# Attention and mixture of experts on one core: the opening of the kernel written out by hand on four engines, and the later key tiles prepared two by two

## The chip, the core and the metric

The kernel runs on one core of a Trainium2 chip. The metric is the device time of one execution in microseconds (us); lower is better. The core has five engines that work side by side: TensorE (PE, matrix products and transposes, with its weight loads shown as PEld), VectorE (DVE), ScalarE (ACT), GpSimd (POOL), and SyncE (SP), which here only issues transfers. Each works through its own queue in order and waits on semaphores for the others.

## The reference

There are 2 batches of 1024 tokens of width 256, all in float32. A small conditioning vector gives six rows for each batch: shifts, scales and gates.

```python
mod = (silu(c) @ wmod).reshape(2, 6, 1, -1)
sa, ca, ga, sb, cb, gb = (mod[:, i] for i in range(6))   # then |ga|, |gb| >= 0.25
h = layernorm(x) * (1 + ca) + sa
xn = layernorm(h) * g_norm
q = l2norm(heads(xn @ Wq) * 16) * 4            # 16 heads of 128
k, v = split(xn @ Wkv)                         # one key and one value head for all
k = l2norm(k) * 4
o = softmax(q @ k.T) @ v
x = x + ga * (layernorm(merge(o) @ Wout) * g_out)
h = layernorm(x) * (1 + cb) + sb
x = x + gb * moe(h)                            # 8 experts, the best 2 for each token
```

## The kernel before

Tokens lie in 16 tiles of 128 (8 for each batch). The attention runs over 4 blocks of 512 query tokens. In a block every head goes over 8 key tiles; one such step is a score matmul (L478), an exponential on ACT (L482), a matmul with the values (L493) and a running sum on DVE (L498). `attention` walks 128 steps, with the scores two steps ahead (`AHEAD`), and at given steps it calls other work that `besides` holds: `at(h, j, f)` puts `f` ahead of step `h * 8 + j`. For block 0 the first sixteen steps are laid out so that two heads go over the first four keys and then over the last four (L809 to L811).

A tile gets its keys in stages. `prep_norm` makes both layer norms on DVE: statistics (L187, L188), then L357 and L360, statistics again, then L367. The inverse root of each is taken on POOL in `rsqrt`, by a scale (L177) and a power (L178). `key_value` transposes the tile on PE (L377), copies it out on ACT with `g_norm` as its scale (L379), and multiplies it by the key and value weights (L384). `normalised_keys` squares the keys on ACT (L399), takes `rsqrt` on POOL and scales them on DVE (L403); `prep_key` transposes them (L420) and copies them to `kT` (L421). Queries come in units of one token tile by four heads: `Queries.make` multiplies (L441) and calls `normalised` (square on ACT L343, sum on DVE L344, `rsqrt` on POOL, product on DVE L347), and `turn` transposes them (L455) and copies them out (L464).

Before the attention starts, lines 777 to 802 prepare the first four tiles: their norms by pairs, their keys, and group 0 of the queries (heads 0 to 3) of block 0. `warm` (L768) issues matmuls of ones whose results nobody reads. Tiles 4 to 7, the other half of the first batch's keys, are prepared one by one beside steps 0 to 5.

Nothing fixes the order of instructions on an engine except the order in which the program names them, dependencies, and a scheduler that fills each engine's queue at build time from what it holds to be ready. `tc.issue_after(ins)` makes what it encloses stand behind `ins` on the engine of `ins`.

Three buffers (`ps_s`) in PSUM hold scores, two (`ps_o`) hold outputs and three (`ps_m`) hold everything else. Outside the beginning the keys of tiles 8 to 15 are still made one by one beside heads 8 to 15 of block 0.

Of the kernel before, what the change touches and what calls it, by code (L numbers as in the profile page):

```python
# [55 lines left out]
def tile_adaln_attention_moe(  # L56
# [75 lines left out]
    wmod_in = wmod.rearrange("(c p) n -> p c n", p=P)  # L132
    wq_in = wq.rearrange("(c p) n -> p c n", p=P)
    nc.sync.dma_start(out=cT_sb, in_=cT.rearrange("(c p) b -> p c b", p=P))
    for t in range(PAIR):
        nc.sync.dma_start(out=xs[:, t, :], in_=xt[:, t, :])
    nc.sync.dma_start(out=wmod_sb[:, :, : 2 * D], in_=wmod_in[:, :, : 2 * D])
    for t in range(PAIR, QT):
        nc.sync.dma_start(out=xs[:, t, :], in_=xt[:, t, :])
    nc.sync.dma_start(out=gn_col, in_=g_norm.rearrange("(c p) -> p c", p=P))  # L140
    nc.sync.dma_start(out=wkv_sb, in_=wkv.rearrange("(c p) n -> p c n", p=P))
# [33 lines left out]
    def rsqrt(out, src, scale, add):  # L175

        nc.gpsimd.tensor_scalar(out, src, scale, add, ALU.mult, ALU.add)  # L177
        latest["pool"] = nc.gpsimd.tensor_tensor(  # L178
            out, out, minus_half[:, : out.shape[1]], ALU.pow
        ).ins  # L180
# [47 lines left out]
    with ExitStack() as attn:  # L228
# [109 lines left out]
        def normalised(src, n, scale, name):  # L338


            sq = work.tile([P, n, DH], FP, tag="sq", name=f"sq_{name}", bufs=1)
            rn = small.tile([P, n], FP, tag="rn", name=f"rn_{name}")
            nc.scalar.activation(sq, src, AF.Square)  # L343
            nc.vector.tensor_reduce(rn, sq, AX.X, ALU.add)  # L344
            rsqrt(rn, rn, 1.0 / ROOT_SCALE**2, L2_EPS / (scale * ROOT_SCALE) ** 2)
            vn = work.tile([P, n, DH], FP, tag=f"vn{n}", name=f"vn_{name}")
            nc.vector.tensor_tensor(  # L347
                vn, src, rn.unsqueeze(2).to_broadcast([P, n, DH]), ALU.mult
            )
            return vn  # L350

        z_of, kn_of = {}, {}
# [16 lines left out]
            )  # L369
            z_of[t] = z  # L370

        def key_value(t, pool, tag):

            z = z_of.pop(t)
            tp = ps_m.tile([P, DC, P], FP, tag="mm", name=f"tp_{t}")
            for c in range(DC):
                nc.tensor.transpose(tp[:, c, :], z[:, ts(c, P)], ident)  # L377
            for c in range(DC):
                nc.scalar.activation(  # L379
                    hT[:, t, c, :], tp[:, c, :], AF.Copy, scale=gn_col[:, c : c + 1]  # L380
                )
            kv = pool.tile([P, 2, DH], FP, tag=tag, name=f"kv_{t}")
            for c in range(DC):
                nc.tensor.matmul(  # L384
                    kv.rearrange("p a d -> p (a d)"),
                    hT[:, t, c, :],
                    wkv_sb[:, c, :],
                    start=(c == 0),
                    stop=(c == DC - 1),
                )  # L390
            nc.scalar.copy(vs[:, t, :], kv[:, 1, :])
            return kv

        def normalised_keys(tiles, kvs):

            rn = small.tile([P, QT], FP, tag="rn", name=f"rnk_{tiles[0]}")[:, : len(tiles)]
            for i, kv in enumerate(kvs):
                sq = work.tile([P, HG, DH], FP, tag="sq", name=f"sqk_{tiles[i]}", bufs=1)
                nc.scalar.activation(sq[:, 0, :], kv[:, 0, :], AF.Square, accum_out=rn[:, i : i + 1])  # L399
            rsqrt(rn, rn, 1.0 / ROOT_SCALE**2, L2_EPS / ROOT_SCALE**2)  # L400
            for i, kv in enumerate(kvs):
                kn = work.tile([P, DH], FP, tag="vn1", name=f"vnk_{tiles[i]}")
                nc.vector.tensor_scalar(kn, kv[:, 0, :], rn[:, i : i + 1], None, ALU.mult)  # L403
                kn_of[tiles[i]] = kn
# [7 lines left out]
            norm_again(t, h, mv, rs, 0)  # L412

        def prep_kv(t):
            normalised_keys([t], [key_value(t, ps_m, "mm")])

        def prep_key(t):

# [8 lines left out]
        class Queries:  # L427


            def __init__(self, blk):  # L430
                self.blk = blk
                self.groups = []
                self.units = [(g, i) for g in range(NG) for i in range(QT)]
                self.made = []

            def make(self, pool=ps_m, tag="mm"):
# [13 lines left out]
            def turn(self, only_act=False):  # L450

                g, i, qn = self.made.pop(0)
                tp = ps_m.tile([P, HG, P], FP, tag="mm", name=f"qp_{self.blk}_{i}_{g}")
                for j in range(HG):
                    nc.tensor.transpose(tp[:, j, :], qn[:, j, :], ident)  # L455
                if i == 0:
                    self.groups.append(
                        big.tile([P, HG, QB], FP, tag="qT", name=f"qT_{self.blk}_{g}", bufs=NG + 1)
                    )
                dst = self.groups[g][:, :, ts(i, P)]  # L460
                if i % 2 and not only_act:
                    nc.vector.tensor_copy(dst, tp)
                else:
                    nc.scalar.copy(dst, tp)  # L464

            def head(self, h):
                return self.groups[h // HG][:, h % HG, :]

        def attention(blk, q, steps, besides):
# [5 lines left out]

            def score(h, j):
                s = ps_s.tile([P, QB], FP, tag="s", name=f"s_{blk}_{h}_{j}")
                nc.tensor.matmul(  # L478
                    s, kT[:, ts(b * NJ + j, P)], q.head(h), start=True, stop=True
                )  # L480
                p = work.tile([P, QB], FP, tag="p", name=f"p_{blk}_{h}_{j}", bufs=4)
                nc.scalar.activation(p, s, AF.Exp)  # L482
                probs[h, j] = p

            def gather(h, j):
                p = probs.pop((h, j))
                if j == 0:
                    outs[h] = ps_o.tile([P, QB], FP, tag="o", name=f"o_{blk}_{h}")
                    sums[h] = work.tile(
                        [P, QB], FP, tag="sum", name=f"sum_{blk}_{h}", bufs=HG + 1  # L490
                    )
                    probs[h] = p
                nc.tensor.matmul(  # L493
                    outs[h], vs[:, b * NJ + j, :], p, start=(j == 0), stop=(j == NJ - 1)
                )
                if j:
                    first = probs.pop(h) if j == 1 else sums[h]
                    latest["vector"] = nc.vector.tensor_tensor(sums[h], first, p, ALU.add).ins  # L498
                if j == NJ - 1:
                    nc.scalar.copy(q.head(h), outs.pop(h))  # L500
# [273 lines left out]
                )  # L774


        q = Queries(0)
        pairs = [list(range(t, t + PAIR)) for t in range(0, QT, PAIR)]
        first = [statistics(small, [xs[:, t, :] for t in ts2], PAIR, f"p{ts2[0]}") for ts2 in pairs]
        warm(3, "a")  # L780
        modulate_in(0)
        warm(5, "b")
        second, hs = [], {}
        for ts2, (mv, rs) in zip(pairs, first):
            both = work.tile([P, QB], FP, tag="p", name=f"h_{ts2[0]}", bufs=4)
            for i, t in enumerate(ts2):
                hs[t] = both[:, ts(i, D)]
                norm_in(t, hs[t], mv, rs, i)
            second.append(statistics(small, [hs[t] for t in ts2], PAIR, f"n{ts2[0]}"))
        for n, (ts2, (mv, rs)) in enumerate(zip(pairs, second)):  # L790
            for i, t in enumerate(ts2):
                norm_again(t, hs[t], mv, rs, i)
            normalised_keys(ts2, [key_value(t, ps_o, "o") for t in ts2])
            for t in ts2:
                q.make(ps_s, "s")
            if n:
                for t in ts2:
                    q.turn(True)
            for t in ts2:
                prep_key(t)  # L800
        for t in ts2:
            q.turn(True)

        HALF = NJ // 2
        settle = None
        for blk in range(NBLK):
            steps = [(h, j) for h in range(HEADS) for j in range(NJ)]
            if blk == 0:
                steps[: 2 * NJ] = [  # L809
                    (h, j + k) for k in (0, HALF) for h in range(2) for j in range(HALF)  # L810
                ]  # L811
            besides = {n: [] for n in range(len(steps))}

            def at(h, j, f, *a):
                besides[h * NJ + j].append(lambda: f(*a))

            after = Queries(blk + 1) if blk + 1 < NBLK else None
            for h in range(HEADS):
                src = q if h < HEADS - HG else after
                if src is not None:  # L820
                    at(h, 0, src.make)
                    at(h, 4, src.turn)
            if settle is not None:
                for i in range(QT):
                    at(1 + i, 2, settle.logits, i)
                at(1 + QT, 2, settle.weights)
                at(1 + QT, 4, count, blk - 1, filled[0], work, ps_m, "mm")
            if blk == 0:
                for i, t in enumerate(range(QT, TPB)):
                    at(0, i, prep_norm, t)  # L830
                    at(0, i + 1, prep_kv, t)
                    at(0, i + 2, prep_key, t)
                for b in range(B):
                    at(2 + b, 3, gate_a, b)
                    at(2 + b, 6, gate_b, b)
                at(4, 4, tables)
                at(5, 3, modulate_moe, 0)
                at(5, 6, modulate_in, 1)
# [272 lines left out]
```

## Time and profile before

| | us |
|---|---|
| runs shown, median of 3 (lowest to highest) | 1354.47 (1352.8 to 1355.57) |
| the profiled execution | 1353.75 |
| its span, first to last instruction | 1352.0 |
| PE busy in the span | 1322.1 (98%) |
| DVE, ACT, POOL busy | 685.4, 489.4, 229.1 |
| first score matmul starts | 41.55 |

The span is what the profile sees; 1.75 us of the profiled execution lie around it. The chain of waits that ended last is followed back from the last instruction, and PE holds 93% of it. "PEclk" is the share of full clock that TensorE was granted. Matmuls of float32 show as two records each, and the ends of matmul records are modelled, so their durations overlap; spacing from start to start is the safer reading: 0.86 us for a matmul of 512 columns at full clock, 0.43 us for one of 256. Timelines and chains give the start and the length of each piece in us from the start of the span, with the engine, the line of the program and what is written from what.

### The profile page before, as it was taken

What the parts mean: (1) busy time and instruction counts of PE and PEld (TensorE: products, weight loads), DVE (VectorE), ACT (ScalarE), POOL (GpSimd) and SP (SyncE); (2) the same over time, 40 slices, a digit from 0 to 9 for tenths busy, and PEclk for the clock granted to TensorE, in tenths of its full rate; (3) what the DMA queues carried; (4) which work ended last, traced back from release to release, by engine and by line L of the source; (5) the groups of instructions that cost most, each with busy time, mean ns of one, the idle gap of its engine ahead of it and who ended that gap; (6) DMA issues with size and microseconds to landing.
All of it is one profiled execution on the core that took longest, in us unless ns stands there. A gap on an engine that the chain in (4) does not pass through costs nothing.

```text
span 1352.0 us, 12731 instructions
## 1 busy us (share of the span) xinstructions
PE 1322.1 (98%) x4024; PEld 686.6 (51%) x4024; DVE 685.4 (51%) x1380; ACT 489.4 (36%) x954; POOL 229.1 (17%) x325
## 2 busy tenths in 40 slices
PE   7899999999999999999999999999999999999995
PEld 3444444446644444447444444457444444476774
DVE  6356655544535554542636353544546544437645
ACT  2433344442243433330343333321333333304442
POOL 4200212110100111000100000001000224003633
PEclk9899999999999999999999999999999999999998
DMA  7000000000003410000001200100001013013435
GB/s 245 1 0 19 13 15 18 1 31 32 1 1 121 93 32 0 31 1 32 0 1 32 86 32 0 32 1 32 1 0 32 26 54 103 31 32 119 135 123 194
DMA packets 46322, 59.18 MB, mean 44 GB/s; under 512 B 10672, under 2 KB 32432, under 8 KB 46256
## 3 DMA queue, kind: packets, MB, share of 16 engines
q1 hardware_dynamic: 42512, 48.08, 11.6%
q0 software_dynamic: 3744, 10.29, 2.1%
q8 instruction: 33, 0.54, 0.2%
q14 instruction: 33, 0.27, 0.1%
HBM read 39.69 MB, written 18.66 MB: 43 GB/s over the span
## 4 chain that ended last, share of the span: by engine, by line
PE 93%; DVE 2%; DMA 2%; POOL 2%; issue 1%; ACT 0%; SPq 0%; POOLq 0%; DVEq 0%; ACTq 0%
PE s L478 32%; PE o L493 32%; PE pr L547 8%; PE q L441 8%; PE su L928 3%; PE sy L959 2%; PE qp L455 2%; PE den L507 1%; DMA out_dram<-res 1%; PE kv L384 1%; PE ap L944 1%; PE xp L913 1%; POOL rn_q L178 0%; PE lg L625 0%; DMA wmod_sb<-in_wmod_dram 0%
## 5 line engine op out<-in xcount | busy, mean ns | idle before, releaser
L478 PE MATMUL s<-qT,kT 128*128 128x512 f32 x1024 | 525.5, 595 | 0.1
L493 PE MATMUL o<-p,vs 128*128 128x512 f32 x1024 | 522.7, 593 | 0.0
L482 ACT ACTIVATE p<-s 128x512 f32<-128x512 f32 x512 | 305.6, 597 | 502.4 <-PE s L478 497.3
L498 DVE TENSOR_TENSOR sum<-sum,p 128x512 f32<-128x512 f32 x384 | 264.5, 689 | 180.2 <-ACT p L482 175.5
L493 PEld LDWEIGHTS o<-p,vs 128*128 128x128 f32 x1024 | 193.5, 190 | 233.2 <-issue 232.1
L478 PEld LDWEIGHTS s<-qT,kT 128*128 128x128 f32 x1024 | 187.4, 191 | 206.0 <-issue 204.1
L177 POOL TENSOR_SCALAR rn_q<-rn_q 128x4 f32<-128x4 f32 x64 | 14.0, 219 | 721.1 <-DVE rn_q L344 706.0
L441 PE MATMUL q<-wq_sb,rows 128*128 128x512 f32 x256 | 121.0, 596 | 0.0
L547 PE MATMUL pr<-wout_sb,qT 128*128 128x256 f32 x512 | 112.7, 381 | 0.0
L547 PEld LDWEIGHTS pr<-wout_sb,qT 128*128 128x128 f32 x512 | 96.7, 190 | 18.8 <-issue 4.3
L498 DVE TENSOR_TENSOR sum<-p,p 128x512 f32<-128x512 f32 x64 | 44.2, 691 | 113.4 <-ACT p L482 113.3
L344 DVE TENSOR_REDUCE rn_q<-sq_q 128x4 f32<-128x512 f32 x64 | 43.8, 684 | 84.0 <-ACT sq_q L343 83.9
L178 POOL TENSOR_TENSOR rn_q<-rn_q,minus_half 128x4 f32<-128x4 f32 x64 | 83.3, 1302 | 5.3
L441 PEld LDWEIGHTS q<-wq_sb,rows 128*128 128x128 f32 x256 | 49.1, 192 | 60.5 <-issue 50.5
L347 DVE TENSOR_TENSOR vn_q<-q,rn_q 128x512 f32<-128x512 f32 x64 | 44.2, 690 | 58.2 <-POOL rn_q L178 58.2
L343 ACT ACTIVATE sq_q<-q 128x512 f32<-128x512 f32 x64 | 38.2, 597 | 75.1 <-PE q L441 70.8
L523 DVE TENSOR_TENSOR qT<-qT,wide 128x512 f32<-128x512 f32 x64 | 42.2, 690 | 44.5 <-DMA wide<-spread 44.2
L515 DVE RECIPROCAL rden<-den 128x512 f32<-128x512 f32 x16 | 53.7, 3358 | 20.0 <-PE den L507 20.0
L928 PE MATMUL su<-w_sb,xT 128*128 x184 | 62.9, 462 | 0.2
L970 POOL DMA_INDIRECT results<-ysb,x x46 | 46.4, 1009 | 54.2 <-DVE ysb L967 37.9
L455 PEld LDWEIGHTS qp<-ident,vn_q 128*128 128x128 f32 x256 | 32.3, 143 | 37.3 <-issue 31.2
L959 PE MATMUL sy<-w2s,sactT 128*128 x184 | 47.2, 380 | 0.0
(160 smaller groups left out, 763.4 us busy)
## 6 DMA issues: line engine op xcount, KB each, us to landing
wide<-spread SPq DMA_DIRECT2D x64, 256.0 KB
x<-sorted_x SPq DMA_DIRECT2D x46, 130.0 KB
y<-results SPq DMA_DIRECT2D x16, 256.0 KB
sorted_x<-zero SPq DMA_DIRECT2D x1, 4030.0 KB
w_sb<-in_w_dram SPq DMA_DIRECT2D x2, 1408.0 KB
wout_sb<-in_wout_dram SPq DMA_DIRECT2D x1, 2048.0 KB
out_dram<-res SPq DMA_DIRECT2D x16, 128.0 KB
sorted_x<-zero SPq DMA_DIRECT2D x1, 1950.0 KB
```

The costliest lines, as they stand in the source:

```text
L178: latest["pool"] = nc.gpsimd.tensor_tensor(out, out, minus_half[:, : out.shape[1]], ALU.pow).ins
L441: nc.tensor.matmul(q.rearrange("p h d -> p (h d)"), hT[:, self.blk * QT + i, c, :], wq_sb[:, c, ts(g, QB)], start=(c == 0), stop=(c == DC ...
L455: nc.tensor.transpose(tp[:, j, :], qn[:, j, :], ident)
L478: nc.tensor.matmul(s, kT[:, ts(b * NJ + j, P)], q.head(h), start=True, stop=True)
L482: nc.scalar.activation(p, s, AF.Exp)
L493: nc.tensor.matmul(outs[h], vs[:, b * NJ + j, :], p, start=(j == 0), stop=(j == NJ - 1))
L498: latest["vector"] = nc.vector.tensor_tensor(sums[h], first, p, ALU.add).ins
L515: nc.vector.reciprocal(rden, den)
L547: nc.tensor.matmul(ps, q.head(h)[:, ts(i, P)], wout_sb[:, h, :], start=(h == 0), stop=(h == HEADS - 1),)
L928: nc.tensor.matmul(u, self.xT[:, c, :], w1_flat[:, c * I2 :][:, bass.ds(at, I2)], start=(c == 0), stop=(c == DC - 1),)
L959: nc.tensor.matmul(y, self.actT[:, c, :], w2_flat[:, c * D :][:, bass.ds(at, D)], start=(c == 0), stop=(c == 1),)
L970: ins = nc.gpsimd.indirect_dma_start(out=results[self.i], out_offset=bass.IndirectOffsetOnAxis(ap=self.x[:, TO : TO + 1].bitcast(I32), axi ...
```

## The change

The loads that open the kernel are reordered: the first third of `wmod` (what `modulate_in` needs) is issued ahead of all four first tiles of `x`, instead of between the second and the third. The rest of the beginning is rewritten.

- The four helpers of a tile are split, so that transposing, multiplying, copying the values and measuring lengths can be named apart (`transposed`, `key_value`, `value`, `key_lengths`, `lengths`, `scaled`). With `both`, half of a tile's copy out after the transpose is on DVE and half on ACT.
- The preparation of tiles 0 to 3 stands in `tc.manual_schedule` for PE, DVE, ACT and POOL: on each of these engines the instructions inside run in the order in which they are written. The norms of tiles 4 and 5 are written in between.
- Group 0 of the queries is made by two token tiles and two heads at a time (`some_queries`, into a buffer of `ps_s`; `turn_some`). Heads 0 and 1 are finished for all four tiles before the first score; heads 2 and 3 of the lower two tiles are multiplied ahead of it (`q_more`) and finished beside step 3; those of the upper two tiles are made beside step 9 and turned beside step 13.
- An exponential of one column is issued early on ACT. `warm` has 3, 7 and 1 matmuls in place of 3 and 5.
- Tiles 6 and 7 have their norms traced at step 0, behind the last query product of the beginning on DVE. The keys of tiles 4 and 5, then of 6 and 7, are made in pairs, each piece behind the attention's latest matmul on PE (`on_tensor`).
- The first sixteen steps go over keys in three parts: 0 to 3, 4 and 5, 6 and 7, for two heads each.
- Group 1 of block 0's queries is made beside steps 11, 16, 21 and 25 instead of 0, 8, 16 and 24.

```diff
-    for t in range(PAIR):
-        nc.sync.dma_start(out=xs[:, t, :], in_=xt[:, t, :])
     nc.sync.dma_start(out=wmod_sb[:, :, : 2 * D], in_=wmod_in[:, :, : 2 * D])
-    for t in range(PAIR, QT):
+    for t in range(QT):
         nc.sync.dma_start(out=xs[:, t, :], in_=xt[:, t, :])
...
+                if both and c:
+                    nc.vector.tensor_scalar(
+                        hT[:, t, c, :], tp[:, c, :], gn_col[:, c : c + 1], None, ALU.mult
+                    )
+                else:
+                    nc.scalar.activation(
+                        hT[:, t, c, :], tp[:, c, :], AF.Copy, scale=gn_col[:, c : c + 1]
+                    )
...
         q = Queries(0)
...
+        def some_queries(tiles, h0):
+            u = ps_s.tile([P, PAIR, PAIR, DH], FP, tag="s", name=f"q_{tiles[0]}_{h0}")
+            for i, t in enumerate(tiles):
+                for c in range(DC):
+                    nc.tensor.matmul(
+                        u[:, i].rearrange("p h d -> p (h d)"),
+                        hT[:, t, c, :],
+                        wq_sb[:, c, h0 * DH : (h0 + PAIR) * DH],
+                        start=(c == 0),
+                        stop=(c == DC - 1),
+                    )
+            return u.rearrange("p i h d -> p (i h) d")
+
+        def turn_some(tiles, h0, vn):
+            tp = ps_m.tile([P, PAIR, PAIR, P], FP, tag="mm", name=f"qp_{tiles[0]}_{h0}")
+            for h in range(PAIR):
+                for i in range(PAIR):
+                    nc.tensor.transpose(tp[:, h, i, :], vn[:, i * PAIR + h, :], ident)
+            dst = q.groups[0][:, h0 : h0 + PAIR, tiles[0] * P : (tiles[0] + PAIR) * P]
+            nc.scalar.copy(dst.rearrange("p h (i k) -> p h i k", k=P), tp)
...
+        with tc.manual_schedule(engines=engines):
+            warm(3, "a")
+            x_low = statistics(small, [xs[:, t, :] for t in low], PAIR, "p_low")
+            x_high = statistics(small, [xs[:, t, :] for t in high], PAIR, "p_high")
+            modulate_in(0)
+            none = small.tile([P, 1], FP, name="none", bufs=1)
+            nc.scalar.activation(none, ones[:, 0:1], AF.Exp)
+            warm(7, "b")
+            h_low = first_norm(low, *x_low)
+            n_low = statistics(small, h_low, PAIR, "n_low")
+            h_high = first_norm(high, *x_high)
+            second_norm(low, h_low, *n_low)
+            n_high = statistics(small, h_high, PAIR, "n_high")
+            for t in low:
+                transposed(t, True)
+            kv_low = [key_value(t, ps_o, "o") for t in low]
+            for t, kv in zip(low, kv_low):
+                value(t, kv)
+            rk_low = key_lengths(low, kv_low)
+            second_norm(high, h_high, *n_high)
+            x_mid = statistics(small, [xs[:, t, :] for t in middle], PAIR, "p_mid")
+            for t in high:
+                transposed(t, True)
+            q_low = some_queries(low, 0)
+            normalised_keys(low, kv_low, rk_low)
+            rq_low = lengths(q_low, HG, SCALE, "q_low")
+            kv_high = [key_value(t, ps_o, "o") for t in high]
+            for t in low:
                 prep_key(t)
-        for t in ts2:
-            q.turn(True)
-
-        HALF = NJ // 2
+            for t, kv in zip(high, kv_high):
+                value(t, kv)
+            rk_high = key_lengths(high, kv_high)
+            q_high = some_queries(high, 0)
+            both = work.tile([P, QB], FP, tag="p", name="h_mid", bufs=4)
+            h_mid = [both[:, ts(i, D)] for i in range(PAIR)]
+            norm_in(middle[0], h_mid[0], *x_mid, 0)
+            vn_low = scaled(q_low, HG, rq_low, "q_low")
+            rq_high = lengths(q_high, HG, SCALE, "q_high")
+            norm_in(middle[1], h_mid[1], *x_mid, 1)
+            turn_some(low, 0, vn_low)
+            q_more = some_queries(low, PAIR)
+            n_mid = statistics(small, h_mid, PAIR, "n_mid")
+            warm(1, "c")
+            vn_high = scaled(q_high, HG, rq_high, "q_high")
+            anchor = latest["multiplied"]
+            turn_some(high, 0, vn_high)
+            normalised_keys(high, kv_high, rk_high)
+            for t in high:
+                prep_key(t)
+            second_norm(middle, h_mid, *n_mid)
...
+        def on_tensor(f, *a):
+
+            with tc.issue_after(latest["tensor"]):
+                f(*a)
...
+        FIRST = ((0, NJ // 2), (NJ // 2, NJ // 2 + PAIR), (NJ // 2 + PAIR, NJ))
...
-                    (h, j + k) for k in (0, HALF) for h in range(2) for j in range(HALF)
+                    (h, j) for j0, j1 in FIRST for h in range(2) for j in range(j0, j1)
...
-                    at(h, 0, src.make)
-                    at(h, 4, src.turn)
+                    late = (11, 8, 5, 1)[h] if not blk and h < HG else 0
+                    at(h, late, src.make)
+                    at(h, late + 4, src.turn)
...
-                for i, t in enumerate(range(QT, TPB)):
-                    at(0, i, prep_norm, t)
-                    at(0, i + 1, prep_kv, t)
-                    at(0, i + 2, prep_key, t)
+                at(0, 0, norms_of_last)
+                at(0, 0, on_tensor, turn_rows, middle)
+                at(0, 1, on_tensor, keys_of, middle)
+                at(0, 3, finish_low)
+                at(0, 5, on_tensor, turn_keys, middle)
+                at(0, 5, on_tensor, turn_rows, last)
+                at(0, 6, on_tensor, keys_of, last)
+                at(1, 2, on_tensor, turn_keys, last)
+                at(1, 1, make_rest)
+                at(1, 5, turn_rest)
```

## The prediction

> **What bounds the kernel.** I read the chain of waits first: PE holds 93% of it. The page says the same:
>
> ```profile
> PE 1322.1 (98%) x4024; PEld 686.6 (51%) x4024; DVE 685.4 (51%) x1380; ACT 489.4 (36%) x954; POOL 229.1 (17%) x325
> ```
>
> The change touches the first 65 us, so I cut that stretch into windows (window: length, then busy us of PE, PEld, DVE, ACT and POOL with counts, the granted clock, DMA):
>
> ```profile
> 10.00:20.00 10.00, 8.46 (x27) 4.32 (x26) 8.69 (x30) 2.80 (x11) 4.81 (x11) 1.00 1.03 373
> 20.00:30.00 10.00, 7.46 (x24) 4.86 (x23) 5.98 (x14) 3.03 (x13) 5.78 (x13) 0.83 0.73 226
> 30.00:40.00 10.00, 4.89 (x21) 3.13 (x20) 5.82 (x16) 3.09 (x7) 5.55 (x12) 0.74 0.00 0
> 40.00:50.00 10.00, 10.00 (x23) 4.57 (x22) 2.95 (x5) 5.78 (x11) 2.21 (x4) 0.75 0.01 2
> 50.00:60.00 10.00, 8.94 (x32) 4.52 (x30) 3.32 (x8) 5.27 (x18) 2.48 (x6) 1.00 0.00 1
> ```
>
> PE idles until about 40, and from 20 to 45 much of what it does runs at half clock. A wider window, 200 to 320, has PE busy 120.00 of 120. So what is saved before the flow is dense is saved at the end, and no later event stands at a fixed time to take it back. PE's timeline gives the point where dense work starts (start, length, what, idle before):
>
> ```profile
> 36.27 1.09 PE L455 MATMUL qp<-ident,vn_q 128*128 128x128 f32 x4 [2.08 <-DVE vn_q L347]
> 38.97 1.09 PE L455 MATMUL qp<-ident,vn_q 128*128 128x128 f32 x4 [1.60 <-DVE mv_n L188]
> 39.85 1.92 PE L441 MATMUL q<-wq_sb,rows 128*128 128x512 f32 x2
> 41.55 3.59 PE L478 MATMUL s<-qT,kT 128*128 128x512 f32 x4
> ```
>
> The last line is two scores: 3.6 us where two cost 1.72 at full clock. What holds PE until then is in the chain, POOL and DVE in turn:
>
> ```profile
> 32.93 0.20 POOL rs_p L177
> 33.13 0.07 issue
> 33.20 0.54 POOL rs_p L178
> 33.74 0.08 issue
> 33.82 0.50 POOL rn_q L177
> 34.32 0.07 issue
> 34.39 1.02 POOL rn_q L178
> ```
>
> The query's inverse length waits behind tile 5's (`rs_p`), which no score needs yet. DVE likewise does norms of later tiles between pieces that PE waits for. The written order goes at this.
>
> **What must be done anyway.** By 65.43 tiles 0 to 7 are ready. From 39.85 to 65.43 are 25.6 us. PE lost 1.5 in gaps (0.48, 0.19, 0.62, 0.19, ahead of the `kp` transposes) and 2.5 to the half clock (0.85 on half a query unit, 1.66 on two scores). So 21.6 us of PE work at full clock.
>
> Work before 39.85 against work ahead of the new first score: both have `s_c`, four tiles' rows, values and keys. The new one makes three quarters of group 0 (not four: 1.72 fewer) and turns two quarters (not four: 2 x 0.44 fewer). That is 2.6 us left for later. If the first score starts at T, the work of 65.43 is done at T + 2.6 + 21.6 + stalls, and the gain is 65.43 - 24.2 - T - stalls = 41.2 - T - stalls.
>
> **T, part by part.** Durations are rows of before: statistics of a tile 0.55 (3.79 to 4.96 for two), norm pass 0.45 (two passes a tile), L367 0.35, L403 0.33, sum L344 0.62, product L347 0.66, square 0.6, copy out of four transposes 0.58, ACT values and lengths 0.17 + 0.37 a tile; POOL 1.15 for two columns and 1.45 for four, hops included.
>
> *The loads.* SP issues `wmod` second, at 1.30 instead of 2.26; five issues move past each other and none is added. It took 4.60 from issue to landing with 256 KB of `x` ahead of it, so at the latest 5.9. At the earliest 5.0: the first `x` tile needed 2.5 to its first use, and three more such tiles' worth take 0.4 each (`wmod` 6.86, next tile used 7.26). The four `x` tiles follow 0.4 apart, the last at 6.6 to 7.5 (before, used by 7.83). I carry 5.9 through the walk.
>
> *DVE from there.* Statistics of four tiles end 8.5; `one_ca` 8.94 (before 9.43). Norms of low 10.8, their statistics 11.9, norms of high 13.7, L367 of low 14.4, statistics of high 15.5. PE: `s_c` to 7.65, seven warm matmuls 6.02 to 13.67; then the first transposes at 14.1 (before 14.68). So the load order buys half a microsecond; the two extra warm matmuls (1.72) lie in PE idle time, and would cost only if L367 were done before 13.67.
>
> *Copies out on two engines.* DVE has two of 0.33 after its statistics, 15.5 to 16.16; ACT alone takes 1.14 for the four (15.16 to 16.3). This is worth nothing or a loss of 0.3 here, since DVE comes late; nearest row: L403, the same kind of operation from PSUM, 0.35.
>
> *Low keys and queries.* kv ends 17.2, the query product of heads 0 and 1 runs 17.65 to 19.4. DVE: L367 of high waits for POOL to 16.65, ends 17.35, statistics of tiles 4 and 5 to 18.45, two scales to 19.1, low keys scaled 19.45 to 20.1 (POOL's `rnk`, after ACT's lengths at 18.3), sum of low queries 20.24 to 20.86, norm of tile 4 to 21.76, product of low queries 22.32 to 22.98 (after POOL's four columns).
>
> *High.* kv of high needs the `ps_o` buffers that the low keys free: 19.9 to 21.6. Its queries 21.8 to 23.5, square 23.7 to 24.3, sum to 25.0, POOL to 26.45. DVE meanwhile does tile 5's norm and both tiles' statistics to 27.0: this later work overruns POOL by 0.55. Product 27.67, transposes 28.2, copy 28.4 to 29.0. **T is 29.0** with the late `wmod`, 28.1 with the early one; I take 28.8, nearer the row. DVE works 20 of those 23 us: it becomes the bound of the beginning.
>
> *The exponential ahead.* The table load is 1.28 us on ACT in both kernels; at 40.70 it hid under the slow score (waited for until 43.5), now it hides in ACT's gap before 14. Worth 0.
>
> *After T.* Each pair's rows, keys and `rsqrt` are spread over several steps. Two tiles' copies out take 1.17 of ACT, an exponential 0.6, and PE has a score and an output, 1.72, to cover them. The pieces that can stand bare are the transposes of tiles 6 and 7 (a third `ps_m` buffer waits for a copy of 0.3) and the key copies just ahead of score 12 (0.3 to 0.5). `q_more` holds one score buffer until its product: two remain, and a score needs one back after 0.6 of exponential, inside 1.72 of other work. Behind a waiting `on_tensor` piece stand the attention's matmuls, and behind those every exponential; before, four such waits cost 1.5. The bounds are 0 and 3; I take 1.0, since two pairs stop PE half as often as four tiles. Group 1 later is free: its last turn is two steps (1.7 to 3.4 us) ahead of use, against a copy of 0.6. `group`, `latest` and the split helpers add no instructions.
>
> *The clock.* It changed at 24.5, 27.9, 34.75 and 45.0: multiples of 3.4 apart. The stretch 21.1 to 24.5 had four transposes (0.44) and nothing else, and half clock followed. [...] That speaks against this change: from the warm matmul's end (26.5) to the first score (29.0) there are only transposes. [...] By the rows, windows of about a tenth busy halved the clock and none near a third is shown; a halving costs half of 3.4 us, 1.7. I take 0, and keep 1.7 for the range.
>
> Sum: gain 41.2 - 28.8 - 1.0 = 11.4. Against its own execution 1353.75 - 11.4 = 1342.3; that execution lies 0.7 under the median shown, so against the median **1343.0**.
>
> **Rivals.** A measurement tells about 0.2% (2.7 us) from no change.
>
> *A, the clock or the waits move along.* As above, but the gap before the first score fills a window (1.7 us), or norms of tiles 6 and 7 slip among the last DVE pieces, or step waits reach 3. For it: DVE's overrun already sits there. [...] 2 to 4 us less: about 1345.7.
>
> *B, everything early.* `wmod` lands at 5.0 and no step stalls: T 28.1, gain 13.1, 1341.4. Against: copies on ACT do compete.
>
> *C, the written order blocks and the time is longer.* In a fixed queue one late piece holds all behind it. If low and high don't overlap at all, one pair's way from its transposes to its queries' copy is 12.4 us (0.44, 0.6, 1.87, 1.08, 1.1, 0.66, 0.66, 1.72, 0.6, 0.62, 1.4, 0.66, 0.44, 0.58 in order); two make 24.9, the middle norms 5.1 and `q_more` with its warm matmul 2.6. From 14.1 that is T = 46.7, a loss of 6.5: 1361. It decides from T = 40.2, 11 us past my walk. Against: PE and ACT in the walk have room to work on one pair while POOL serves the other.
>
> *D, the order isn't kept or half works.* T near 34: 1348.5.
>
> **Chances.** Main 0.55, own range 1341.8 to 1344.6. A 0.22, B 0.13, D 0.06, C 0.04. The range 1340.5 to 1346.8 holds main, B and most of A, leaving out C, D and A's tail. Faster by over 0.2% 0.95 (all but C and a corner of D), within 0.02, slower 0.03.
>
> **What would show it.** First score at 28 to 29.5; last product of the beginning at about 27, with DVE the engine that sets it; PE gaps after the first score of about 1 in sum; clock 1.00 throughout from 5 us on. Score and output counts are unchanged, and the stretch from the end of tile 7's keys to the end is as long as before. Wrong: a first score after 31, a half-clock stretch after it, or PE gaps later than 65 us that before didn't have.

## The result and the profile after

The changed kernel takes 1346.34 us (median of 6 runs, 1345.55 to 1347.16), the kernel before 1353.32 beside it: a ratio of 0.9948, 95% interval [0.9937, 0.9958], or 7.0 us less. The forecast was 1343.0, 11.4 less than the runs then shown; the range of 1340.5 to 1346.8 holds the result near its upper end, where it had been stretched to take in most of rival A; the main case's own range, 1341.8 to 1344.6, does not reach it. The profiled span fell from 1352.0 to 1344.7.

The same windows after the change (length, busy us of PE, PEld, DVE, ACT and POOL, granted clock, DMA):

```profile
10.00:20.00 10.00, 9.16 (x36) 5.31 (x35) 8.43 (x28) 3.17 (x12) 3.67 (x8) 1.00 1.02 388
20.00:30.00 10.00, 8.02 (x39) 6.05 (x38) 7.58 (x21) 3.40 (x13) 4.84 (x9) 1.00 0.69 214
30.00:40.00 10.00, 8.53 (x27) 4.38 (x25) 6.43 (x18) 5.46 (x16) 4.21 (x10) 1.00 0.01 2
40.00:50.00 10.00, 8.27 (x24) 4.49 (x25) 2.65 (x4) 3.85 (x10) 0.95 (x1) 0.83 0.00 1
50.00:60.00 10.00, 10.00 (x32) 5.74 (x31) 3.43 (x8) 4.05 (x11) 0.94 (x3) 1.00 0.00 0
```

PE is dense 12 us earlier than before, but not from the first score on: 30 to 50 has a hole. PE's timeline shows both ends of it:

```profile
27.93 0.63 PE L822 MATMUL qp<-ident,vn_q_high 128*128 128x128 f32 x4 [1.52 <-DVE vn_q_high L351]
28.39 0.38 PE L440 MATMUL kp<-ident,vnk 128*128 128x128 f32 x2
29.23 1.98 PE L502 MATMUL s<-qT,kT 128*128 128x512 f32 x4 [0.46 <-ACT qT L824]
...
37.51 1.02 PE L517 MATMUL o<-p,vs 128*128 128x512 f32 x2
41.73 1.11 PE L822 MATMUL qp<-ident,vn_q_more 128*128 128x128 f32 x4 [3.20 <-DVE vn_q_more L351]
42.63 1.92 PE L502 MATMUL s<-qT,kT 128*128 128x512 f32 x2
44.34 1.41 PE L517 MATMUL o<-p,vs 128*128 128x512 f32 x2
45.59 1.02 PE L502 MATMUL s<-qT,kT 128*128 128x512 f32 x2
```

The first score starts at 29.23, against 41.55. After 37.51 PE waits 3.20 us for the product that the transposes of `q_more` need, at step 3, and then works slowly: from start to start the transposes take 0.90 (0.44 elsewhere), the score 1.71 and the output 1.25 (0.86 each), 1.7 us too many. The clock windows name the reason (third number from the end):

```profile
39.00:40.00 1.00, 0.00 (x0) 0.00 (x0) 0.81 (x2) 0.00 (x0) 0.62 (x2) 1.00 0.00 0
40.00:41.00 1.00, 0.00 (x0) 0.00 (x0) 0.02 (x1) 0.00 (x0) 0.95 (x1) 1.00 0.00 0
...
42.00:43.00 1.00, 1.00 (x5) 0.97 (x5) 0.00 (x0) 0.12 (x1) 0.00 (x0) 0.50 0.00 0
43.00:44.00 1.00, 1.00 (x2) 0.34 (x1) 0.00 (x0) 0.46 (x1) 0.00 (x0) 0.50 0.00 0
44.00:45.00 1.00, 1.00 (x2) 0.34 (x1) 0.00 (x0) 0.41 (x1) 0.00 (x0) 0.50 0.00 0
```

What held the product? POOL's timeline, and DVE's for the same stretch:

```profile
36.09 0.19 POOL L175 TENSOR_SCALAR rs_p<-mv_p 128x1 f32<-128x1 f32 x1 [1.55 <-DVE mv_p L186]
36.37 0.55 POOL L176 TENSOR_TENSOR rs_p<-rs_p,minus_half 128x1 f32<-128x1 f32 x1
37.00 0.19 POOL L175 TENSOR_SCALAR rnk<-rnk 128x2 f32<-128x2 f32 x1
37.27 0.70 POOL L176 TENSOR_TENSOR rnk<-rnk,minus_half 128x2 f32<-128x2 f32 x1
39.30 0.56 POOL L175 TENSOR_SCALAR rn_q_more<-rn_q_more 128x4 f32<-128x4 f32 x1 [1.32 <-DVE rn_q_more L345]
39.94 1.01 POOL L176 TENSOR_TENSOR rn_q_more<-rn_q_more,minus_half 128x4 f32<-128x4 f32 x1
```

```profile
38.01 0.61 DVE L420 TENSOR_SCALAR vnk<-kv,rnk 128x128 f32<-128x128 f32 x2 [2.00 <-POOL rnk L176]
38.53 0.67 DVE L345 TENSOR_REDUCE rn_q_more<-sq_q_more 128x4 f32<-128x512 f32 x1
39.13 0.68 DVE L522 TENSOR_TENSOR sum<-sum,p 128x512 f32<-128x512 f32 x1
40.98 0.69 DVE L351 TENSOR_TENSOR vn_q_more<-q,rn_q_more 128x512 f32<-128x512 f32 x1 [1.17 <-POOL rn_q_more L176]
```

The squares of `q_more` were ready at 36.3 (on ACT, 35.70 and 0.60 long). Their sum (L345) stands behind the keys' scales (L420) in DVE's queue, those wait for POOL's `rnk`, and on POOL `rs_p`, the norm of tile 8, which DVE first uses at 144.7, stands ahead of `rnk`. It is the pattern of the kernel before, moved to the first steps.

### The profile page after: what moved, and what is told of

It reads as the page before. It is cut to its first block, busy times and chain, and to the rows that moved or that the text cites. A ratio compares the mean times of both kernels' runs of the same rounds, so it can differ in the third digit from the quotient of the medians.

```text
span 1344.7 us, 12754 instructions
## 1 busy us (share of the span) xinstructions
PE 1320.7 (98%) x4046; PEld 688.4 (51%) x4046; DVE 686.7 (51%) x1384; ACT 488.2 (36%) x951; POOL 225.1 (17%) x313
## 3 DMA queue, kind: packets, MB, share of 16 engines
q1 hardware_dynamic: 42512, 48.08, 11.5%
## 4 chain that ended last, share of the span: by engine, by line
PE 94%; DVE 2%; DMA 2%; POOL 1%; issue 0%; ACT 0%; SPq 0%; POOLq 0%; DVEq 0%; ACTq 0%
PE s L502 32%; PE o L517 32%; PE q L462 8%; PE pr L571 8%; PE su L1069 4%; PE sy L1100 3%; PE qp L476 2%; PE den L531 1%; PE kv L396 1%; PE ap L1085 1%; PE xp L1054 1%; PE lg L649 0%; DMA y<-results 0%; DMA wide<-spread 0%; DMA xs<-in_x_dram 0%
## 5 line engine op out<-in xcount | busy, mean ns | idle before, releaser
L462 PE MATMUL q<-wq_sb,rows 128*128 128x512 f32 x240 | 112.8, 592 | 0.0
L345 DVE TENSOR_REDUCE rn_q<-sq_q 128x4 f32<-128x512 f32 x60 | 41.1, 685 | 84.4 <-ACT sq_q L344 84.2
L176 POOL TENSOR_TENSOR rn_q<-rn_q,minus_half 128x4 f32<-128x4 f32 x60 | 79.4, 1323 | 4.9
L462 PEld LDWEIGHTS q<-wq_sb,rows 128*128 128x128 f32 x240 | 45.5, 190 | 56.9 <-issue 46.4
L351 DVE TENSOR_TENSOR vn_q<-q,rn_q 128x512 f32<-128x512 f32 x60 | 41.4, 690 | 54.0 <-POOL rn_q L176 54.0
```

The source lines that it names most:

```text
L176: latest["pool"] = nc.gpsimd.tensor_tensor(out, out, minus_half[:, : out.shape[1]], ALU.pow).ins
L462: nc.tensor.matmul(q.rearrange("p h d -> p (h d)"), hT[:, self.blk * QT + i, c, :], wq_sb[:, c, ts(g, QB)], start=(c == 0), stop=(c == DC ...
```

## Experiments

The first four ran on a chip where the kernel before takes 1353.1; the others on chips where it takes 1358.1 and 1357.8. So times are compared as ratios to the kernel before on the same chip, and a first score is compared by its distance from the first transposes (`tp`), since the start of the kernel shifts by about 1 us from one execution to the next (the first `tp` of the changed text starts anywhere from 13.64 to 14.66).

**split_turn: only the transposes of step 3 go to step 7.**

```diff
-            turn_some(low, PAIR, normalised(q_more, HG, SCALE, "q_more"))
+            made["more"] = normalised(q_more, HG, SCALE, "q_more")
+
+        def turn_low():
+            turn_some(low, PAIR, made["more"])
...
                 at(0, 3, finish_low)
+                at(0, 7, turn_low)
```

> Only the transposes of the lower tiles' second query half move, from step 3 to step 7; their length and product stay traced at step 3. Theory S: what the forecast missed is one PE wait of 3.2 us ahead of these transposes (38.5 to 41.7) and the half-clock window that follows it (1.9 us). Then both go: 5.1 us less than the changed kernel's 1346.3, so 1341.2, no PE gap over 0.5 us after the first score and clock 1.00. Rival R: PE waits at step 3 for something that step 5 needs as well (the pair's keys, or a score buffer that the unfinished queries hold), so the wait moves on: at most 1.5 us less, about 1345, with a gap of 2 to 3 us at step 5 or 7.

Measured: 1341.59, ratio 0.9920 [0.9907, 0.9933]. PE's timeline at the old place and at the new one:

```profile
38.38 1.02 PE L517 MATMUL o<-p,vs 128*128 128x512 f32 x2
39.23 1.02 PE L502 MATMUL s<-qT,kT 128*128 128x512 f32 x2
...
48.49 0.60 PE L822 MATMUL qp<-ident,vn_q_more 128*128 128x128 f32 x4
48.92 1.02 PE L502 MATMUL s<-qT,kT 128*128 128x512 f32 x2
```

No idle time stands ahead of any PE row from the first score to 60 us. The granted clock reads 1.00 in every window from 0 to 200. Wait and slow window are gone together, 4.8 us by the medians (3.8 by the ratios), and nothing waits in their place.

**norm_behind: tiles 8 to 15 have their norms behind the latest running sum.**

```diff
+        def norm_behind(t):
+            with tc.issue_after(latest["vector"]):
+                prep_norm(t)
...
-                    at(h, 1, prep_norm, t)
+                    at(h, 1, norm_behind, t)
```

> Only the norms of tiles 8 to 15 are held behind the attention's latest running sum on DVE, so that tile 8's statistics can't be pulled forward to 33.4 us. Theory S says that its scale and power on POOL (36.09 to 36.92), ahead of the keys' (37.0), hold the keys' scaling and, in DVE's order, the length of the queries that PE waits for: POOL was free for the keys from 35.7, so the PE wait shrinks from 3.2 by about 1.2 to 2.0. If that gap no longer halves the clock, 3.1 us less, 1343.2; if it still does, 1345.1. Rival R: the chain of the queries' own square, sum, power and product sets the wait and tile 8 has no part: same time, 1346.3, gap still 3.2.

Measured: 1343.77, ratio 0.9932 [0.9919, 0.9945]. PE's timeline:

```profile
41.20 0.66 PE L822 MATMUL qp<-ident,vn_q_more 128*128 128x128 f32 x4 [1.96 <-DVE vn_q_more L351]
41.69 1.02 PE L502 MATMUL s<-qT,kT 128*128 128x512 f32 x2
```

The wait is 1.96 instead of 3.20, and the score after it takes 0.86: tile 8's norm on POOL was 1.2 us of the wait. In this profile the clock stays at 1.00 behind the shorter gap; but no_order below has the same gap, 1.96, with a halving behind it.

**warm_gap: three unread matmuls ahead of the wait.**

```diff
+                at(0, 3, on_tensor, warm, 3, "d")
                 at(0, 3, finish_low)
```

> Three more matmuls of ones, whose result nobody reads, stand on PE just ahead of the waiting transposes of step 3. Theory S: they fill 2.6 us of a 3.2 us wait, cost nothing, and keep the clock: 1.9 us less, 1344.4, transposes still at about 41.7 and clock 1.00 after them. Rival: the slow rows after the wait are not the clock's doing, or the matmuls push the transposes back: no gain or up to 1 us more, 1346.3 to 1347.3.

Measured: 1344.49, ratio 0.9942 [0.993, 0.9955]. The transposes start at 41.92, 12.6 us after the first score (12.5 in the changed kernel), and the score after them at 42.38 takes 0.86. The work fills the wait, the clock stays at 1.00 behind it, and only the slow window goes: 1.85 us by the medians, 0.8 by the ratios, whose intervals overlap. The profile shows it; the times alone wouldn't.

**no_order: the same text without the manual schedule.**

```diff
-        with tc.manual_schedule(engines=engines):
+        with ExitStack():
```

> The beginning is written as in the changed kernel, but outside a manual schedule: the build's scheduler orders the four engines. Theory of the forecast: the order itself carries most of the early first score, since without it norms of later tiles come ahead of pieces that PE waits for on DVE and POOL as before the change: first score at 33 to 36 instead of 29.2, 1350 to 1353 in all. Rival: naming the pieces in this sequence, by pairs and half groups, is what counts and the scheduler keeps about the same order: first score within 1 us of 29.2, 1345 to 1347.5.

Measured: 1347.03, ratio 0.9951 [0.9939, 0.9963], which can't be told from the changed kernel's 0.9948. The first score stands 16.3 us behind the first transposes instead of 15.44. My expectation of 33 to 36 was wrong: naming the pieces by pairs and halves in this sequence brings nearly all of the early first score, and fixing the queues 0.85 us. Even these are spent again at step 3, where PE waits 1.96 us instead of 3.20: without the fixed order tile 8's norm is through POOL by 35.5, before the keys' lengths are there at 38.9.

```profile
43.73 0.66 PE L822 MATMUL qp<-ident,vn_q_more 128*128 128x128 f32 x4 [1.96 <-DVE vn_q_more L351]
44.23 1.45 PE L502 MATMUL s<-qT,kT 128*128 128x512 f32 x2
45.47 1.92 PE L517 MATMUL o<-p,vs 128*128 128x512 f32 x2
```

The clock falls at 44.7 here, behind a gap as long as norm_behind's, and it has fallen once before, at 31.0 on the first scores. This profiled execution is the slowest of its six (1343.56 to 1348.09). So no gain of the fixed order shows.

**loads_back, one_engine, no_warm_c: three parts undone in split_turn.** In turn: the two `x` loads again ahead of `wmod`; `transposed(t, False)` for low and high; the line `warm(1, "c")` taken out.

> split_turn (the changed kernel with the transposes of step 3 at step 7, 1341.6) with the order of the first loads as before the change: wmod behind two tiles of x. Theory of the forecast's walk: the conditioning product starts at 7.0 instead of 5.5, the second norms' chain on DVE starts about 1.1 us later and everything behind follows: first score and total 0.9 to 1.5 us later, about 1342.8. Rival: DVE has slack further on (it waits for POOL at 16 and 22), so the load order is hidden: 1341.6.

Measured: ratio 0.9917 [0.9904, 0.9931]; split_turn had 0.9920, and 0.9926 in a second set. In the times the load order is worth nothing that shows. The rows of the conditioning product, here and then in the changed kernel:

```profile
6.37 1.96 PE L248 MATMUL s_c<-wmod_sb,scb 128*128 128x512 f32 x4 [0.61 <-DMA wmod_sb<-in_wmod_dram]
```

```profile
5.50 1.95 PE L246 MATMUL s_c<-wmod_sb,scb 128*128 128x512 f32 x4
```

With `wmod` first, the product no longer waits for it, but it still stands behind the three warm matmuls on PE, and these end anywhere from 5.4 to 6.4 from one execution to the next. In split_turn's own profile it started at 6.39, no earlier than here. In split_again's the warm matmuls end early, the product starts at 5.79 and the first `tp` at 13.64, against 14.29 here: in such an execution the load order can be worth the forecast's half microsecond. The distance from the first `tp` can't show that, since `tp` itself moves.

> split_turn with all four copies out after a pair's transposes on ACT instead of two on DVE. Theory of the forecast: worth nothing, since DVE's copies stand behind statistics and end at 15.5, when ACT alone would be done at about 15.4: 1341.6 within 0.3, or slightly less because DVE sheds 1.2 us. Rival: the two engines do halve the wait of PE: first score 0.6 us later, 1342.2 or more.

Measured: ratio 0.9912 [0.9897, 0.9928]. The first score stands 14.77 us behind the first transposes instead of 15.44. Two engines for the copies don't help: they add 1.2 us to DVE, for whose last product PE waits 1.52 us in split_turn and 1.12 here, and cost 0.67 of first score; in the times the intervals overlap.

> split_turn without the one matmul of ones ahead of the last transposes before the first score. PE then has only transposes for 3.8 us instead of 2.8. [...] If a window that is mostly idle does it too, the clock falls in most: up to 1.7 us more, 1342.8 to 1343.3, with scores of half speed at the first steps.

Measured: ratio 0.9928 [0.9914, 0.9942]. The windows of its profile:

```profile
26.00:27.00 1.00, 0.00 (x0) 0.00 (x0) 0.94 (x4) 0.00 (x0) 0.98 (x1) 1.00 0.39 112
27.00:28.00 1.00, 0.00 (x0) 0.00 (x0) 0.68 (x2) 0.00 (x0) 0.63 (x2) 1.00 0.01 4
28.00:29.00 1.00, 0.66 (x6) 0.66 (x6) 1.00 (x5) 0.00 (x0) 0.25 (x1) 1.00 0.03 8
29.00:30.00 1.00, 0.54 (x3) 0.30 (x2) 1.00 (x5) 0.92 (x3) 0.00 (x0) 1.00 0.00 0
30.00:31.00 1.00, 1.00 (x2) 0.33 (x1) 1.00 (x5) 0.00 (x0) 0.59 (x2) 0.59 0.06 16
31.00:32.00 1.00, 1.00 (x3) 0.46 (x2) 0.41 (x2) 0.60 (x1) 0.57 (x1) 0.50 0.00 0
```

The clock falls at 30.2, and in the 3.4 us ahead of it PE wasn't idle throughout: it was busy for 1.36, with transposes and half a microsecond of scores. In time, 0.9928 can't be told from split_turn's 0.9920 and 0.9926.

**before_hold: one edit to the kernel before.** The norms of tiles 4 to 7 stand behind the last query product of the beginning (`anchor`).

```diff
+        def norm_behind(t):
+            with tc.issue_after(anchor):
+                prep_norm(t)
...
-                    at(0, i, prep_norm, t)
+                    at(0, i, norm_behind, t)
```

> The kernel before, with one edit: the norms of tiles 4 to 7 are held on DVE behind the last query product of the beginning (as the change does for tiles 6 and 7); no other order is written and all else is as before. Theory: what kept the first score at 41.6 were these norms on DVE and POOL (about 11 us of the chain of waits between 16 and 39), so it comes at 32 to 34, and the keys' norms still arrive in time for most steps: 1343.5 to 1346, about as fast as the whole change. Rival: the keys are needed soon after, so PE waits for the same norms at the steps instead: first score early, but PE gaps of 6 us or more behind it, 1349 to 1353.

Measured: ratio 0.9996 [0.9988, 1.0005], no change. PE's timeline:

```profile
36.55 1.96 PE L478 MATMUL s<-qT,kT 128*128 128x512 f32 x4
...
43.73 1.02 PE L478 MATMUL s<-qT,kT 128*128 128x512 f32 x2
48.19 0.47 PE L420 MATMUL kp<-ident,vnk 128*128 128x128 f32 x1 [3.44 <-DVE vnk L403]
```

The first score comes 5.0 us earlier (5.4 by the distance from the first `tp`), not 8, and PE then waits 3.44 us for tile 4's key, and behind it, to 54.00, its rows take twice their time: from start to start the output at 48.88 and the score at 52.29 take 1.71 each (0.86 elsewhere). Here the rival held: norms that are only put off are waited for at the next step.

**whole_group, two_parts, best, with split_turn again as split_again beside them.** whole_group makes, turns and copies out heads 0 to 3 ahead of the first score, without `warm_c`; two_parts restores keys 0 to 3 and 4 to 7; best joins split_turn, norm_behind and one_engine.

> split_turn once more, as a reference on the same chip for the other three: 0.992 of the kernel before, as measured, between 0.9907 and 0.9933.

> The changed kernel with all of group 0 (heads 0 to 3, four tiles) made, turned and copied out on PE ahead of the first score, in the written order; the unread matmul gives way to the last query product. No half is left for the steps. Theory: the first score waits for two more chains of length, POOL and product and comes 3.5 to 4 us later, against 2.6 us of PE work less afterwards: 1.0 to 1.4 us more than split_again, and 1.7 to 3.4 more if the clock halves in the 6 us of transposes: ratio 0.993 to 0.9955. Rival: the halves only move work about, since PE must do it all anyway: within 0.4 of split_again.

> split_turn with the first sixteen steps over keys in two parts again (0 to 3, then 4 to 7), and the transposes of the keys of tiles 6 and 7 two steps earlier, ahead of the scores that now need them. Theory: the third part buys the chain of these keys (value, length, POOL, scale: about 3.5 us after their product) two more steps; without it PE waits 1.5 to 2 us ahead of the key transposes, so 1.2 to 2 us more than split_again. Rival: the chain is done in the two steps that remain (3.4 us) and the part is worth nothing: within 0.4 of split_again.

> split_turn with all copies out after the transposes on ACT and tile 8's norms held behind the running sums. The first gave a first score 0.67 us earlier after the first transposes (14.77 against 15.44), the second took 1.2 us off a wait that is gone here. Theory: 0.7 us less than split_again, the lowest of all. Rival: with the wait gone neither lies on PE's path any more: within 0.3 of split_again.

split_again has 0.9926 [0.9912, 0.9939]. whole_group has 0.9954 [0.9941, 0.9968], 3.8 us more. PE's timeline:

```profile
33.58 1.09 PE L822 MATMUL qp<-ident,vn_q_more 128*128 128x128 f32 x4 [4.74 <-DVE vn_q_more L351]
34.84 1.09 PE L822 MATMUL qp<-ident,vn_q_rest 128*128 128x128 f32 x4 [0.18 <-DVE vn_q_rest L351]
35.73 3.25 PE L502 MATMUL s<-qT,kT 128*128 128x512 f32 x4
```

The first score stands 21.9 us behind the first transposes, 6.45 later where 3.5 to 4 was expected, against 2.6 us of PE work saved afterwards: 3.85, close to the measured 3.8. Both waits, for the chain and for the clock, are in it (the four transposes of `q_rest` take 0.89 from start to start instead of 0.44); the half clock behind the first score, about 1.7 in split_again's profile and 1.3 in this one, is not. The halves are worth 3 to 4 us.

two_parts has 0.9923 [0.9909, 0.9936], and no PE gap up to the last key transposes: the rival held, the third part of the keys is worth nothing that shows. best has 0.9909 [0.9894, 0.9925], the lowest; its first score stands 14.78 us behind the first transposes, as expected. In time it is 2.3 us under split_again, more than the expected 0.7, and the intervals overlap. In split_again's profile the clock had fallen just at the first scores (PEclk is the third number from the end):

```profile
28.00:29.00 1.00, 0.64 (x6) 0.42 (x4) 1.00 (x4) 0.54 (x2) 0.00 (x0) 1.00 0.00 0
29.00:30.00 1.00, 0.90 (x1) 0.50 (x2) 1.00 (x6) 0.38 (x3) 0.22 (x1) 0.53 0.00 0
30.00:31.00 1.00, 1.00 (x3) 0.37 (x2) 0.47 (x2) 0.00 (x0) 0.92 (x2) 0.50 0.07 16
```

In best's profile its first two scores take 1.82 us to the next row, against 3.48 there. But that execution is the slowest of best's four (1347.45, the others 1345.54 to 1345.63), so the whole spans say little. Up to the first division by `den` the profiles can be compared without what comes later:

```profile
13.79 0.73 PE L381 MATMUL tp<-ident,z 128*128 128x128 f32 x4 [0.33 <-DVE z L371]
...
117.46 1.07 PE L531 MATMUL den<-sum,ones 128*32 128x512 f32 x8
```

```profile
14.66 0.73 PE L381 MATMUL tp<-ident,z 128*128 128x128 f32 x4
...
113.27 1.07 PE L531 MATMUL den<-sum,ones 128*32 128x512 f32 x8
```

These are the changed kernel and split_turn. The same two rows in every run, with the half clock between them counted in windows of 3.4 us (by the granted clock, and in before_hold, loads_back, two_parts, one_engine, best and whole_group by the rows that take twice their time):

| run | from first `tp` to first `den`, us | half-clock windows |
|---|---|---|
| before, before_hold | 110.52, 108.99 | 4, 3 |
| the changed kernel | 103.67 | 1 |
| split_turn, loads_back | 98.61, 98.62 | 0, 0 |
| split_again, two_parts, no_warm_c | 100.29, 100.31, 100.31 | 1, 1, 1 |
| norm_behind, warm_gap | 100.80, 102.09 | 0, 0 |
| no_order | 105.03 | 2 |
| one_engine, best | 97.94, 97.95 | 0, 0 |
| whole_group | 103.71 | 2 |

With 1.7 taken off for a window, split_again, two_parts and no_warm_c are split_turn to 0.1 us. One engine for the copies is worth 0.67, and norm_behind adds nothing to it: best's 2.3 us under split_again are 0.67 of first score and 1.7 of clock in these profiles. The changed kernel is split_turn with 3.36 us of wait (start to start, less 0.86) and 1.7 of clock.

## Why the prediction was right, and where its sum was off

**The frame held.** "What is saved before the flow is dense is saved at the end": the first division by `den` moved from 125.30 to 117.53 (7.8 us), the first output projection from 323.96 to 316.19, the last expert product from 1336.05 to 1328.92 (7.1). About 0.6 of the 7.8 is given back between 324 and 1217. That is more likely the scatter of one execution than a cost of the change: from the first output projection to the last expert product PE's timeline has 1012.25 before and 1012.89 after, and 1012.06 to 1012.48 in the first four experiments, which have the same text there.

**T was walked well.** Forecast 28.8, measured 29.23, in an execution whose warm matmuls ended early (conditioning product at 5.50); in split_turn's, with 6.39, it is 30.10. From the first transposes on, the walk had 14.7 and the profiles have 15.44. The walk's own stations: first transposes 14.1 (13.79), low key scales 19.45 (18.97), keys of high 19.9 (19.47), sum of high queries 24.4 (24.11), their product 27.0 (27.09). DVE's queue sets T, as said: PE's last long wait ahead of the first score, 1.52 us, is for its product; that tile 5's norm and statistics overrun POOL there shows too (26.8 against 26.6).

**The two terms behind T were mis-sized.** The sum was 41.2 - T - stalls, with 1.0 of stalls and 0 for the clock. Measured: 41.2 - 29.2 - 3.2 - 1.7 = 7.1, against 7.0 in the runs. That the two meet so closely is luck, for at the first division the profile has 7.8. The 41.2 was about 0.7 low. It took the four gaps of the kernel before from the idle column, which counts from a matmul's modelled end:

```profile
50.36 1.02 PE L478 MATMUL s<-qT,kT 128*128 128x512 f32 x2
51.86 0.33 PE L420 MATMUL kp<-ident,vnk 128*128 128x128 f32 x1 [0.48 <-DVE vnk L403]
```

From start to start this gap is 1.50 - 0.86 = 0.64, and the four together are 2.15 instead of 1.48. With the wait at step 3 read the same way, 3.36, the sum is 41.9 - 29.2 - 3.4 - 1.7 = 7.6. The step that failed is *After T*: it looked for bare pieces among the key transposes, where PE never waited, and let `q_more` pass for its score buffer alone. Its chain of square, sum, power and product was never walked through the queues as the ones before T were. split_turn shows that this wait and the slow window behind it are the shortfall within the noise: without them the gain is 10.8 us by the ratio and 11.5 by the medians, against 11.4; norm_behind that 1.2 of the wait is tile 8's norm; warm_gap that the slow window is the clock.

**The clock step** gave 1.7 as the price of a halving, which is what the rows gave, but put the danger ahead of the first score. It came behind the wait. It can come at the first place too, as split_again shows. That it would cost 0 there was an estimate, and the profile of before didn't carry it. Of its two falls the step looked at the first, at 24.5; the second, at 34.7, came after 3.4 us in which PE was busy for 1.45 by the windows (31.32 to 34.74), most of it transposes, so that one over a third busy was shown:

```profile
31.51 0.82 PE L455 MATMUL qp<-ident,vn_q 128*128 128x128 f32 x6
32.17 0.27 PE L420 MATMUL kp<-ident,vnk 128*128 128x128 f32 x1
33.86 0.33 PE L420 MATMUL kp<-ident,vnk 128*128 128x128 f32 x1 [1.42 <-ACT qT L464]
```

In no_warm_c and split_again the 3.4 us ahead of the fall are much like these, with PE busy for 1.36 and 1.4: about half a microsecond of dense matmuls and 0.9 of transposes.

**Parts.** The load order was forecast to buy half a microsecond; none shows in the times, and one pair of profiles has 0.65. Copies out on two engines were forecast at 0 to -0.3; they cost 0.67 of first score. Order: the forecast let the written order carry T; no_order gives it 0.85, which the longer wait at step 3 takes back, and before_hold gives 5.0 to holding back later norms, lost again at the keys. What the named steps (`on_tensor`) are worth was not measured.

**Rivals.** A, the waits and the clock move along, is what happened, at 1346.3 where it was put at 1345.7; I had given it 0.22 against 0.55. It had waits of up to 3 at the steps, and there were 3.2; its half-clock window stood ahead of the first score and came behind the wait. Two of the forecast's own signs of being right failed with it: PE gaps of about 1 in sum, and a clock of 1.00 throughout.

## What to carry to other kernels

When work is moved from before the dense stretch to just behind it, walk its chain through every queue up to the step that uses it, as carefully as the path to the first step: a moved piece is a new deadline. Issue what produces a value and what consumes it on the bound engine as two calls, several steps apart; here that alone was worth more than half of what the whole change had brought. And look at what the scheduler has pulled ahead on a side engine: a small operation that nobody needs yet can stand before one on which the bound engine waits.

## What the hardware showed that I hadn't expected

In these profiles the granted clock stayed low for 3.4 us at a time or a multiple of it (3.4 and 10.2 in the kernel before, 3.4 in the changed one). It fell although PE hadn't been idle throughout the 3.4 us ahead: they had 0.5 us of scores and 0.9 of transposes in no_warm_c (to 30.2), 0.4 of warm matmul and 0.9 of transposes in split_again (to 29.1), and 0.3 of an output, 0.5 of transposes and 0.45 of a score in no_order (to 44.7). The length of the gap alone doesn't tell: no_order has one of 1.96 there, and behind the same gap in norm_behind the clock stayed at 1.00; in split_again PE waits 1.53 ahead of the last transposes and the clock falls, in the changed kernel 1.52 and it stays. What decides between them isn't shown. One unread matmul (0.86 us) stood ahead of split_again's gap and didn't keep the clock; three in a gap of 3.2 did in the execution of warm_gap that was profiled.

The kernel's first matmuls are slow for a time that differs from one execution to the next: from the start of the first to the start of the conditioning product the three of `warm_a` take 5.28 us in split_turn's profile and 4.39 in the changed kernel's, where three take 2.58 later on, while the granted clock reads 1.00 in both. This moved the conditioning product between 5.50 and 6.39 and all that follows with it; a difference in first scores below 1 us between two kernels is only seen when both are measured from the same event. More of the scatter goes with the clock: over no_order's six executions the mean granted clock went from 0.993 to 0.997, the fastest (1343.56) had 0.997, and the three slowest (1347.34 to 1348.09) had 0.993.
